# Fetching, transposing and preparing earlier in a fused attention and feed-forward block on one Trainium2 core

## The chip, the cores and the metric

The kernel runs on one core of a Trainium2 chip. The metric is device time in microseconds (us) of one launch. TensorE (PE in the profile) multiplies matrices, VectorE (DVE), ScalarE (ACT) and GpSimd (POOL) work on elements, and SyncE (SP) issues every DMA of this kernel.

## The reference

One transformer block on x of 2048 rows by 1024 columns, all in float32, with 16 heads of 64 columns and a feed-forward part of width 2752 whose weights are four-bit codes with a scale for each 64 entries:

```
x = x + layernorm(attention(layernorm(x), Wq, Wk, Wv, Wo))      # causal, rotary positions on q and k
x = x + layernorm(ffn(layernorm(x)))                            # ffn(x) = (silu(x Wg') * (x Wu')) Wd'
Wg, Wu, Wd = NF4[codes] * scales
```

## The kernel before, in words

Every large product is made of three float32r matmuls on a high and a low part of each operand (`split`: ACT copies the high part, DVE subtracts to get the low part). Rows of x go in four chunks `c` of 512 rows, and in 16 blocks `t` of 128 rows.

The first part is attention. `qkv(m, c, ...)` (L226) makes q, k and v of head pair m for chunk c: 3 products of 24 matmuls each (L236 to L238), with x transposed in `xs` and weights in `w`. After each product ACT copies it to `t1`. q and k get their rotation and go to DRAM (`qs`, `ks`); v is transposed by TensorE at once (`pv`, L250), split and stored to `vs` (L255). Chunk 0 of x is transposed straight into tiles `xc`; `make_x` (L213) transposes the other chunks, stores them to DRAM (`xd`), and `load_x` (L199) fetches all four tiles of a chunk when its first head pair begins. The 32 pairs (m, c) are called groups; the first four are made at the start, the others in `rest`.

Attention proper is a list of 640 units (h, J, kb): head h, chunk J of queries, block kb of 128 keys. For a unit TensorE makes the scores (`s`, L454 and L455), ACT takes the exponential (L458) and a copy (`pw`, L125), DVE subtracts (`pw`, L126), and three units later TensorE multiplies by v (`o`, L478 to L480). `maxima` (`mx`, L420, reduced on DVE at L426) runs ahead to give each row's maximum, which goes into q. The loads are put at steps: `load_q` 4J + 4 + 8 units or less before the head begins, `load_k` 8 units, `load_v` 5 units. When a head ends, `yl` (L484) takes the sums and products to DRAM (`at`).

The generator `rest` (L564) is the filler: its matmuls are drawn between those of the units until `FILL` is met, a table of how many should be spent by which step. A `yield GAP` ends the filler's turn in a step. When its groups are done, `rest` loads and splits the eight tiles of the output projection (`prep_wo`, L490: load `wof`, ACT copy L494, subtraction on DVE or POOL L495), and then projects the blocks t = 0 to 11 (`project_out`; `pj`, L529 to L531). `attended(t)` (L509) loads the heads' products (`af`) and the reciprocals of their sums (`rt`), multiplies and splits them (`ah`, `af`). `reciprocals(J)` (L500) fetches the 16 rows of sums of a chunk with eight DMAs and stores their reciprocals with eight. `residual` adds, normalizes, and the block's `y` goes to DRAM (`yd`).

The second part is the feed-forward: `fill_x2(t)` (L650) loads y and transposes it (`pt`, L153) into tiles `x2`, `gate_up` (L660) makes gate and up products (`bk`, L119 to L121), `gate_up_weights` (L323) and `looked_up` (L290) turn codes into weights (seven ACT lines, L307, and some eleven DVE operations per 512 columns), and `down` makes the last product.

On-chip memory is in slots of fixed size, named in `SLOTS`: for instance `f4` has four of 4 KB a partition (weights `wf` and `wof`, `hl`, `vo`, `af`, `ah`), `pw` three of 4 KB, `ol` one of 2 KB, `xc` four, `pa` six and `w` three of 8 KB. A tile waits until the one that had its slot is no longer read. The order of instructions is made in two steps. The functions above give a priority by the order in which they are called; the tile scheduler then orders each engine's instructions by these priorities and its own timeline of what is ready. TensorE's matmuls in the attention part are chained to the order written. Each engine, SP too, works its instructions in the order of the built program.

Of the kernel before, what the change touches and what calls it, by code (L numbers as in the profile page):

```python
# [21 lines left out]
E = 1024  # L22
D = 64
# [12 lines left out]
MOST = 16  # L36
LAG = 3

FILL = ((-12, 0), (14, 304), (130, 912), (290, 1520), (430, 2128), (438, 2128), (630, 2704))
# [19 lines left out]
def block_kernel(ctx, tc, x, wq, wk, wv, wo, gu_codes, gu_scales, d_codes, d_scales, cos_sin, out):  # L59
# [104 lines left out]
    at = [dram.tile([2 * KE, D + 1, 512], F32, tag=f"at{c}", name=f"at{c}") for c in range(NC)]  # L164
# [34 lines left out]
    def load_x(c):  # L199
        tiles = []  # L200
        for kp in range(4):
            tiles.append(slot("xc", [P, 4, 2, 2, P], FR, "xc"))
            load(f32(tiles[kp]), xd[c][:, kp])
        return tiles
# [8 lines left out]
    def make_x(c, t, xt):  # L213

        xs = slot("pa", [P, 4, 2, 2, P], FR, "xs")
        for g in range(0, KE, 4):
            pt = bank("T", "pt").rearrange("p (k n) -> p k n", k=4)
            for k in range(4):
                yield T.transpose(pt[:, k], xt[:, (g + k) * P : (g + k + 1) * P], ident)
            for k in range(0, 4, 2):  # L220
                split(xs[:, (g + k) // 2, 0], xs[:, (g + k) // 2, 1], pt[:, k : k + 2])
            if g:
                load(xd[c][:, :, t], f32(xs))
            yield GAP

    def qkv(m, c, ws, xs, tab, ramp=False, following=None):  # L226

        cs = slice(c * 512, (c + 1) * 512)
        for n in range(3):
# [16 lines left out]
            if n == 2:  # L246
                yield GAP
                pv = bank("T", "pv").rearrange("p (t n) -> p t n", t=4)
                for t in range(4):
                    yield T.transpose(pv[:, t, :], t1[:, t * P : (t + 1) * P], ident)  # L250
                vo = slot("f4", [P, 2, 4, 2, D], FR, "vo")
                src = pv.rearrange("p t (a d) -> p a t d", a=2)
                for a in range(2):
                    split(vo[:, a, :, 1], vo[:, a, :, 0], src[:, a])
                load(  # L255
                    vs[m][:, :, 4 * c : 4 * c + 4].rearrange("a p t n -> p a (t n)"),
                    f32(vo.rearrange("p a t l d -> p a (t l d)")),
                )
            else:
# [9 lines left out]
                else:  # L269
                    for a in range(2):  # L270
                        load(ks[m][a][:, :, cs].rearrange("a d s -> d a s"), f32(hl[a * D : (a + 1) * D]))
            yield GAP

# [10 lines left out]
    for m in range(STARTUP):  # L284
        ws[m + 2] = [None] * 3 if m + 2 <= STARTUP else None
        for _ in qkv(m, 0, ws[m], xs, tab, True, ws[m + 2] and (ws[m + 2], m + 2, ("w", "pa", "w", "w")[m])):
            pass
        done.add((m, 0))

    def looked_up(codes, s0, s1, rows, tags=None):  # L290

        if tags:
            c8, sc = (slot(tag, [P, 512], F32, "cs") for tag in tags)
        else:
            cs = slot("pw", [P, 2, 512], F32, "cs")
            c8, sc = cs[:, 0], cs[:, 1]
# [4 lines left out]
        l0 = slot("ol" if not tags else "t2", [P, 512], F32, "l0")  # L301
# [21 lines left out]
    def gate_up_weights(it, tags=None):  # L323
# [4 lines left out]
        def columns_of(k0):  # L328
# [4 lines left out]
                gu_codes[:, off : off + n], gu_scales[0:1, off : off + n], gu_scales[1:2, off : off + n], P, tags  # L333
# [137 lines left out]
    def weighted(u, h, J, kb):  # L471
# [11 lines left out]
        y = slot("pw", [D + 1, 512], F32, "yl")  # L483
        A.copy(y, o[: D + 1, :])  # L484
        load(at[J][h], y)
# [14 lines left out]
    def reciprocals(J):  # L500

        r = slot("ol", [P, D], F32, "sums")
        for a in range(8):
            load(r[16 * a : 16 * a + 16], at[J][:, D, a * D : (a + 1) * D])
        V.reciprocal(r, r)
        for a in range(8):
# [368 lines left out]
```

## Time and profile before

| | us |
|---|---|
| median of 3 runs | 3160.05 (3159.8 to 3160.71) |
| profiled execution, its own time | 3161.3 |
| its span | 3159.5 |
| TensorE busy (97%) | 3052.3 |
| DVE busy (66%) | 2097.3 |
| ACT busy (58%) | 1830.8 |
| POOL busy (17%) | 527.9 |

The page of the profile shows busy time per engine, the span cut in 40 slices of 79 us (a digit is the busy share in tenths; PEclk is the clock that TensorE was granted), and the costliest groups. The trace behind it can be asked for waits (who waited for whom), for stretches of time, and for single instructions. A matmul of 512 columns is shown with 0.39 us, but one starts every 0.23 us, since they overlap. The queues moved 554.71 MB, 176 GB/s over the span.

### The profile page before, as it was taken

Reading aid. Unit: us, or ns where it says so; the run is one execution under the profiler, and the core shown is the slowest. Engines: PE = TensorE matmul, PEld = TensorE weight load, DVE = VectorE, ACT = ScalarE, POOL = GpSimd, SP = SyncE. Lnnn points to the kernel's source line nnn. Section 1 sums busy time; section 2 is a strip of 40 time slices with the busy share of each in tenths; the row PEclk is TensorE's granted clock in tenths of the full one; section 3 lists DMA queues with packets and bytes.
Section 4 is the critical chain, followed back from the end, with each engine's and each line's share of the span. In section 5 each row is a group of like instructions: output and inputs, shape, how many; then the busy total and the mean of one; then the engine's idle time right before and its main releaser. Section 6 shows DMA issues by size and latency. Waiting matters only on the chain.

```text
span 3159.5 us, 41575 instructions
## 1 busy us (share of the span) xinstructions
PE 3052.3 (97%) x14272; PEld 2442.6 (77%) x14272; DVE 2097.3 (66%) x3809; ACT 1830.8 (58%) x3318; POOL 527.9 (17%) x430
## 2 busy tenths in 40 slices
PE   8989999999999997999989899999999999999998
PEld 6768777777777775777767788888888888888887
DVE  6646665766666665777776697667766679867322
ACT  3445565666666665666674586556655557657311
POOL 7534333232333321100101000000000000000000
PEclk9999999999999998999999999999999999999999
DMA  6977767766675656667535432222222235867785
GB/s 204 282 231 229 229 185 221 214 183 174 176 203 170 175 152 188 162 168 186 156 116 157 160 120 103 99 100 100 98 93 90 100 107 190 286 212 237 266 296 204
DMA packets 374100, 554.71 MB, mean 176 GB/s; under 512 B 25920, under 2 KB 238912, under 8 KB 358016
## 3 DMA queue, kind: packets, MB, share of 16 engines
q1 hardware_dynamic: 373888, 552.04, 56.8%
q8 instruction: 113, 1.85, 0.2%
q14 instruction: 99, 0.81, 0.1%
HBM read 410.12 MB, written 141.82 MB: 175 GB/s over the span
## 4 chain that ended last, share of the span: by engine, by line
PE 84%; DMA 6%; DVE 5%; ACT 2%; POOL 1%; issue 1%; SPq 1%; DVEq 0%; POOLq 0%; ACTq 0%
PE bk L119 14%; PE bk L120 14%; PE bk L121 14%; PE qkv L236 5%; PE qkv L237 5%; PE qkv L238 5%; PE mx L420 4%; PE s L454 4%; PE s L455 3%; PE o L479 3%; PE o L480 3%; PE o L478 3%; DMA af<-at 2%; PE pj L529 1%; PE pj L530 1%
## 5 line engine op out<-in xcount | busy, mean ns | idle before, releaser
L307 ACT ACTIVATE ln<-cs,bias 128x512 f32<-128x512 f32 x910 | 611.4, 718 | 119.0 <-DVE mp L313 41.5
L426 DVE TENSOR_REDUCE mxs<-mx 128x1 f32<-128x512 f32 (+3 forms) x640 | 386.4, 605 | 230.9 <-PE mx L420 127.7
L119 PE MATMUL bk<-x,wt 128*128 128x512 f32 x1376 | 536.2, 391 | 2.5 <-ACT x L125 2.4
L121 PE MATMUL bk<-x,wt 128*128 128x512 f32 x1376 | 536.3, 390 | 1.2 <-DVE wt L126 1.2
L120 PE MATMUL bk<-x,wt 128*128 128x512 f32 x1376 | 536.6, 390 | 0.0
L458 ACT ACTIVATE s<-s 128x512 f32<-128x512 f32 (+3 forms) x640 | 332.2, 520 | 286.2 <-PE s L455 164.3
L126 DVE TENSOR_TENSOR pw<-s,pw 128x512 fp32r<-128x512 f32 (+3 forms) x640 | 385.7, 606 | 142.0 <-ACT pw L125 137.6
L125 ACT CAST pw<-s 128x512 fp32r<-128x512 f32 (+3 forms) x640 | 333.3, 523 | 70.3 <-PE o L479 56.1
L182 POOL TENSOR_TENSOR w<-wf,w 128x512 fp32r<-128x512 f32 x192 | 250.8, 1317 | 650.1 <-ACT w L181 463.0
L137 POOL TENSOR_TENSOR rs<-ve,nhalf 128x1 f32<-128x1 f32 x64 | 39.4, 616 | 1786.5 <-DVE ve L135 1786.5
L236 PE MATMUL qkv<-xc,w 128*128 128x512 f32 x768 | 307.0, 401 | 1.7 <-ACT t L243 0.8
L237 PE MATMUL qkv<-xc,w 128*128 128x512 f32 x768 | 305.7, 398 | 0.0
L238 PE MATMUL qkv<-xc,w 128*128 128x512 f32 x768 | 304.1, 396 | 0.0
L119 PEld LDWEIGHTS bk<-x,wt 128*128 128x128 f32 x1376 | 258.9, 188 | 57.2 <-ACT x L125 2.9
L121 PEld LDWEIGHTS bk<-x,wt 128*128 128x128 f32 x1376 | 258.9, 188 | 55.2 <-DVE wt L126 1.6
L120 PEld LDWEIGHTS bk<-x,wt 128*128 128x128 f32 x1376 | 259.2, 188 | 53.8
L454 PE MATMUL s<-q,ka 128*128 128x512 f32 (+3 forms) x640 | 242.2, 378 | 21.4 <-DVE pw L126 21.1
L119 PE MATMUL bk<-wd,it 128*128 128x512 f32 x672 | 261.6, 389 | 1.2 <-DMA it<-ind 1.2
L420 PE MATMUL mx<-ka,q 128*128 128x512 f32 (+3 forms) x640 | 243.8, 383 | 18.4 <-DMA q<-qs 12.4
L120 PE MATMUL bk<-wd,it 128*128 128x512 f32 x672 | 261.5, 389 | 0.0
L121 PE MATMUL bk<-wd,it 128*128 128x512 f32 x672 | 261.3, 389 | 0.0
L478 PE MATMUL o<-pw,va 128*65 128x512 f32 (+3 forms) x640 | 235.8, 368 | 0.0
(126 smaller groups left out, 5436.7 us busy)
## 6 DMA issues: line engine op xcount, KB each, us to landing
it<-ind SPq DMA_DIRECT2D x84, 1024.0 KB
ind<-hl SPq DMA_DIRECT2D x84, 512.0 KB
va<-vs SPq DMA_DIRECT2D x160, 256.0 KB
cs<-in_gu_codes SPq DMA_DIRECT2D x86, 256.0 KB
cs<-in_gu_scales SPq DMA_DIRECT2D x172, 128.0 KB
wf<-in_wq SPq DMA_DIRECT2D x32, 512.0 KB
wf<-in_wk SPq DMA_DIRECT2D x32, 512.0 KB
wf<-in_wv SPq DMA_DIRECT2D x32, 512.0 KB
```

The costliest lines, as they stand in the source:

```text
L119: r = T.matmul(o, lhsT=w[:, 0], rhs=xx[:, 0], start=first, stop=False)
L120: T.matmul(o, lhsT=w[:, 0], rhs=xx[:, 1], start=False, stop=False)
L121: T.matmul(o, lhsT=w[:, 1], rhs=xx[:, 0], start=False, stop=last)
L125: A.copy(hi, src)
L126: V.tensor_tensor(lo, src, f32(hi), ALU.subtract)
L236: yield T.matmul(o, lhsT=w[k][:, 0], rhs=xx[0], start=k == 0, stop=False)
L237: yield T.matmul(o, lhsT=w[k][:, 0], rhs=xx[1], start=False, stop=False)
L238: yield T.matmul(o, lhsT=w[k][:, 1], rhs=xx[0], start=False, stop=k == KE - 1)
L307: A.activation(ln, c8, AF.Identity, bias=bias_of[ab], scale=ab[0])
L420: chain(T.matmul(s, lhsT=q[:, 0, j * P : (j + 1) * P], rhs=ka[:, b:e], start=True, stop=not diag))
L426: V.tensor_reduce(mx[:, j, i : i + 1], s, AX.X, ALU.max, negate=True)
L454: chain(T.matmul(s[:, cs], lhsT=ka[:, ks_], rhs=q[:, 0, cs], start=True, stop=False))
```

## The change

Six things change, with the same matmuls in all.

- `load_x(c, kps)` fetches part of a chunk. Two of the four tiles are fetched when head pair 6 of the chunk before begins, into slots given by `X_TAGS` that are free then; the other two and the table when the chunk's own first pair begins. Instead of ten pauses there are two, then 12 matmuls on the first two tiles, then three pauses.
- `qkv` no longer transposes v itself. It returns a generator `values`, which the next group runs after its first product (24 matmuls later).
- `prep_wo` runs in the last groups: tile 0 into `pa` at the last but one, tiles 1 to 3 into `w` after each product of the last, tiles 4 to 7 into `xc` after it, ahead of `attended(0)`.
- `at` is laid out `[D + 1, 2 KE, 512]`, so that the 16 rows of sums of a chunk are adjacent. One DMA fetches them and one stores the reciprocals.
- The last entry of `FILL` moves from step 630 to 643, and y of block 0 is fetched at step 634.
- In the second part, `x2` of chunks 2 and 3 is filled with a `gate_up` between the two. Some tiles change slots: `yl` from `pw` to `ol`, `xs` of `make_x` from one `pa` to two halves in `pw`, the first codes from `ol` and `t2` to `pw`, the sums to a tile of their own.

```diff
+X_TAGS = (("xc",) * 4, ("pa", "pa", "xc", "xc"), ("xc", "xc", "pa", "pa"), ("xc",) * 4)
-FILL = ((-12, 0), (14, 304), (130, 912), (290, 1520), (430, 2128), (438, 2128), (630, 2704))
+FILL = ((-12, 0), (14, 304), (130, 912), (290, 1520), (430, 2128), (438, 2128), (643, 2704))
-    at = [dram.tile([2 * KE, D + 1, 512], F32, tag=f"at{c}", name=f"at{c}") for c in range(NC)]
+    at = [dram.tile([D + 1, 2 * KE, 512], F32, tag=f"at{c}", name=f"at{c}") for c in range(NC)]
...
-    def load_x(c):
+    def load_x(c, kps):
         tiles = []
-        for kp in range(4):
-            tiles.append(slot("xc", [P, 4, 2, 2, P], FR, "xc"))
-            load(f32(tiles[kp]), xd[c][:, kp])
+        for kp in kps:
+            tiles.append(slot(X_TAGS[c][kp], [P, 4, 2, 2, P], FR, "xc"))
+            load(f32(tiles[-1]), xd[c][:, kp])
...
     def make_x(c, t, xt):
-        xs = slot("pa", [P, 4, 2, 2, P], FR, "xs")
         for g in range(0, KE, 4):
+            xs = slot("pw", [P, 2, 2, 2, P], FR, "xs")
...
-            if g:
-                load(xd[c][:, :, t], f32(xs))
+            load(xd[c][:, g // 2 : g // 2 + 2, t], f32(xs))
...
-            if n == 2:
-                yield GAP
-                pv = bank("T", "pv").rearrange("p (t n) -> p t n", t=4)
...
+            if after_n:
+                after_n(n)
             yield GAP
+            if n == 0:
+                yield from before
+
+        def values():
+            pv = bank("T", "pv").rearrange("p (t n) -> p t n", t=4)
+            for t in range(4):
+                yield T.transpose(pv[:, t, :], t1[:, t * P : (t + 1) * P], ident)
...
+            done.add((m, c))
+            yield GAP
+
+        return values()
...
     def reciprocals(J):
-        r = slot("ol", [P, D], F32, "sums")
-        for a in range(8):
-            load(r[16 * a : 16 * a + 16], at[J][:, D, a * D : (a + 1) * D])
+        r = small.tile([P, D], F32, tag="sums", name="sums", bufs=1)
+        load(r, at[J][D].rearrange("h (a d) -> (h a) d", a=8))
         V.reciprocal(r, r)
-        for a in range(8):
-            load(rcp[J][:, a * D : (a + 1) * D], r[16 * a : 16 * a + 16])
+        load(rcp[J].rearrange("h (a d) -> (h a) d", a=8), r)
...
     def rest():
...
             if m == 0:
                 while ("x", c) not in done:
                     yield GAP
-                xs_, tab_ = load_x(c), load_tab(c)
-                for _ in range(10):
+                xs_ = [*ahead, *load_x(c, range(len(ahead), 4))]
+                tab_, ahead = load_tab(c), []
+                for _ in range(2):
                     yield GAP
+            if m == KE - 2 and ("x", c + 1) in done:
+                ahead = load_x(c + 1, range(2))
+            if g == len(groups) - 2:
+                wot[0] = prep_wo(0, "pa")
...
+            def wo_after(n):
+                wot[n + 1] = prep_wo(n + 1, "w")
+
+            one = qkv(
+                m, c, w, xs_, tab_, False, None if last else (following, groups[g + 1][0], "w"), values, wo_after if last else None
+            )
+            if m == 0:
+                for _ in range(12):
+                    yield next(one)
+                for _ in range(3):
+                    yield GAP
+            values = yield from one
             w = following
+        for k in range(4, KE):
+            wot[k] = prep_wo(k, "xc")
+        yield from values
         ready = [attended(0)]
-        for k in range(KE):
-            wot[k] = prep_wo(k, "w" if k < 3 else "xc" if k < KE - 1 else "pa")
-        for _ in range(6):
+        for _ in range(8):
             yield GAP
...
+    put(634, 5, load_y, 0)
...
-    for c in range(2):
-        gate_up(*todo[1], c)
-    new_x2(2, ["w"] * 3 + ["pa"])
-    new_x2(3, ["xc"] * 4)
-    for t in range(8, NT):
-        fill_x2(t)
+    for c, tags in ((2, ["w"] * 3 + ["pa"]), (3, ["xc"] * 4)):
+        new_x2(c, tags)
+        for t in range(4 * c, 4 * c + 4):
+            fill_x2(t)
+        gate_up(*todo[1], c - 2)
```

## The prediction, made before the change was run

> **What bounds the kernel now.** I read the page's busy lines first, then TensorE's waits, then stretches of the trace around those waits.
>
> ```profile
> PE 3052.3 (97%) x14272; PEld 2442.6 (77%) x14272; DVE 2097.3 (66%) x3809; ACT 1830.8 (58%) x3318; POOL 527.9 (17%) x430
> ...
> PE   8989999999999997999989899999999999999998
> ...
> PEclk9999999999999998999999999999999999999999
> ```
>
> TensorE (PE) is the bound: 97% busy, nobody else over 66%. The change has the same matmuls, shape by shape, so it can gain only where TensorE waits, or works at a reduced clock. Both show in the early slices and in two dips, near 1200 us (the page's slice 16) and 1650 us (slices 21 to 23). The view of waits for TensorE (line, what it waited for, us in total, times, longest) says on what:
>
> ```profile
> PE s L454 <- DVE pw L126: 21.1, 23, 3.6
> PE mx L420 <- DMA q<-qs: 12.4, 1, 12.4
> ...
> PE pj L529 <- ACT wo L494: 8.4, 4, 5.2
> PE pt L153 <- DMA y<-yd: 6.6, 2, 4.0
> PE pv L250 <- ACT t L243: 5.7, 3, 2.6
> ...
> PE pt L153 <- DVE hl L678: 3.7, 1, 3.7
> ```
>
> Each is a few long waits, not a steady drip. Asked by stretch (start:end and length, busy and count of PE, PEld, DVE, ACT, POOL, granted clock, DMA share, GB/s):
>
> ```profile
> 76.00:128.00 52.00, 44.21 (x189) 35.47 (x188) 30.43 (x56) 18.23 (x40) 32.14 (x27) 0.88 0.93 271
> 204.00:229.00 25.00, 12.62 (x76) 10.85 (x75) 7.86 (x20) 9.96 (x25) 2.48 (x2) 0.73 0.93 305
> 506.00:524.00 18.00, 14.76 (x77) 10.86 (x75) 10.59 (x22) 11.65 (x27) 2.50 (x2) 0.91 1.05 364
> 1204.00:1249.00 45.00, 28.64 (x92) 18.01 (x91) 17.93 (x28) 19.04 (x30) 9.46 (x4) 0.70 0.78 209
> 1300.00:1600.00 300.00, 292.57 (x1391) 219.53 (x1389) 220.80 (x404) 198.14 (x351) 31.74 (x26) 1.00 0.62 164
> 1618.00:1654.00 36.00, 27.90 (x118) 18.91 (x116) 28.33 (x52) 31.14 (x59) 3.90 (x3) 0.91 0.38 116
> 1654.00:1668.00 14.00, 8.79 (x31) 6.71 (x32) 9.71 (x23) 6.83 (x18) 0.00 (x0) 0.52 0.43 133
> 1691.00:1699.00 8.00, 5.18 (x20) 4.06 (x19) 5.60 (x9) 4.78 (x9) 0.00 (x0) 0.79 0.93 221
> 1764.00:1798.00 34.00, 25.41 (x125) 20.19 (x124) 21.65 (x52) 20.33 (x48) 0.55 (x1) 0.85 0.61 203
> 1840.00:1920.00 80.00, 80.00 (x355) 66.26 (x354) 73.20 (x129) 60.47 (x97) 0.00 (x0) 1.00 0.35 119
> ```
>
> The last row is the yardstick: full clock, no gap, 80/355 = 0.225 us per 512-column matmul. Everything after 1800 us looks so and the change does not enter it, apart from the last waits of the output. In 1204:1249 only 92 matmuls ran, worth at most 92 x 0.225 = 20.7 us: at least 24 of 45 us are lost, of them 45 - 28.64 = 16.4 idle and the rest slow clock.
>
> [...] after a gap of 2.43 us before the `pv` transposes at 81.3 us, a matmul took 0.63 us, where before the gap it took 0.39. So a wait costs more than its length. [...] SP took 11.99 us, from 1217.38, for five `wof` issues. [...] `attended(0)` holds two of the four `f4` buffers while eight `wof` want the rest.
>
> **The change, part by part**, against the profiled span of 3159.5 us (3161.3 us with what lies around the span; the median of the runs is 3160.05, so the profiled execution is a usual one, and the saving is taken off the median).
>
> 1. *v behind the next product.* In 76:128 TensorE idles 52 - 44.21 = 7.8 us and the clock lacks 0.12 x 52 = 6.2 us. Two of the `pv` waits (2.4 and 2.6 us) lie here. With 24 other matmuls (5.4 us) between the copy of `t1` and its transposes, that copy is long done. What is late next is DMA, at 0.93 here. I take **-8** (ends 0 and -13).
>
> 2. *x a group ahead.* In 204:229 TensorE idles 12.4 us; with the slow clock after it some 15 are lost. SP was issuing four 1024 KB loads of x, the k stores and a weight load, so the q load of the next head went out late and took 5.72 us. Two of the four x loads now come earlier, and the order of instructions in the built program has 72 projection matmuls between units 20 and 30 where 24 stood: 48 x 0.225 = 10.8 us of cover. **-10** (-5 to -15). In 506:524, the next row, the same emptiness costs 3.2 idle and 1.6 of clock: **-4** (0 to -5). The third row gives nothing: between 600 and 1190 us TensorE waits 0.4 us in all.
>
> 3. *Projection weights in the last group.* Now each of the eight is a load (3.5 to 6.8 us), an ACT copy (1.04), and a DVE (1.22) or POOL (2.36) subtraction, in two buffers, with `pj` waiting. Moved, they stand in ACT's order between units 428 and 436, and `pj` starts after unit 440: at 2.1 us per unit (300 us for 143 units in 1300:1600) that is over 8 us of lead, before `attended(0)` takes its two buffers. ACT's 8 x 1.04 = 8.3 us then queue before the exponentials, which have room (ACT at 198 of 300). What stays is `ah`, which held ACT 4.07 us for the load of `rt`. Of 24: **-19** (-8 to -24).
>
> 4. *Filler up to unit 643, y of row block 0 early.* From 1618 to 1668 the 149 matmuls are worth at most 33.5 of 50 us: 16 lost. The built order now has 43 `pj` matmuls after unit 630 where 3 stood, 18 of them after the last unit, while y loads. But ACT is at 31 of 36 us there, so the stretch cannot shrink much; what it gives is 40 x 0.225 = 9 us of `pj` taken out of the earlier, full stretch. **-9** (-2 to -16).
>
> 5. *Sums adjacent.* Sixteen small DMAs (SP 3.56 and 3.55 us) become two, ahead of the `ah` that TensorE awaits in 1691:1699, where 2.8 + 1.7 are lost: **-3** (0 to -4.5). The rows of `at` lie 32 KB apart instead of 2; the pieces stay 2048 and 512 bytes, and `af` is loaded 48 matmuls ahead: 0.
>
> 6. *Row blocks 8 to 15 filled between products.* 1764:1798 loses 8.6 idle and up to 5.1 of clock; y of the last blocks stays the late thing. **-5** (+3 to -13).
>
> 7. *What it adds.* Two x loads per row start only when the old x is free; 2 MB at the 305 GB/s of 204:229 is 6.9 us, against 12 matmuls and three pauses. 2 us a row, **+6** (0 to +20). `xs` in the three `pw` buffers may hold ACT until its store lands: **+2** (0 to +10). ACT's copies before exponentials: **+1** (0 to +5). Twelve more xd issues on SP against 56 fewer small ones, and `yl` in `ol`, used once in 4 to 16 units: 0, as SP's pauses hide them.
>
> Sum: -8 -10 -4 -19 -9 -3 -5 +9 = -49, so a span of 3159.5 - 49 = 3110.5, and **3111** as a median (3160.05 - 49).
>
> **Rivals.**
> *The waits half come back* (x late at each row, `wof` late for ACT, DMA full at the start): only items 2, 3 and 4 at their low ends plus half of 7's: -5 -8 -2 -8 +2, about -20: **3140**. For it: DMA shares over 0.9 in three of the stretches. Against: the order gives each load more lead.
> *All goes*: each item at its far end, -90, less 5 added: **3075**. Against: DVE waits like the 21.1 us of `s` stay.
> *Slower: SP's one queue.* In the last group a `wof` at its head waits for a buffer while q, k and v of the next heads stand behind. k goes out 8 units ahead, 8 x 2.1 = 17 us. The hold seen is 12 us, so it hides. It decides from 17 us on, and each head that is then late costs what 204:229 lost, 15 us. Four heads are 60, more than the 49: 3160 + 60 - 49 = **3171**. Against it: four buffers turn over where two did.
> *No effect* would need TensorE's order unchanged, and the built order does differ.
>
> **How the numbers follow.** Forecast 0.70 (own range 3090 to 3132), half back 0.17, all goes 0.08, slower 0.05. The range 3076 to 3150 leaves out the slower case and the ends. Within 0.2% (6 us, about what a measurement of this kernel tells from no change) lies the far edge of the second case, 0.03: faster 0.92, same 0.03, slower 0.05.
>
> **What would show it.** Right: no `q<-qs` wait of 12 us near 205; `pv` waits gone; `wo` gone from TensorE's waits; a clock of 9 in slice 16; steady stretches after 1800 us unchanged. Step 2 fails if `qkv` waits for `xc`, step 3 if `s` waits while ACT waits for `wof`, step 4 if 1618:1668 still idles 13 us. The forecast is wrong if new waits of over 40 us appear.

## The result, and the profile after

The forecast was 3111 us, faster. The changed kernel takes 3170.62 us (median of 9 runs, 3163.15 to 3181.73) against 3162.39 for the kernel before (9 runs, 3159.8 to 3165.3): a ratio of 1.0029, 95% interval 1.0015 to 1.0042. It is slower by 0.3%.

The profiled execution of the changed kernel is its slowest, 3181.73 us with a span of 3180.0, 11 above its median. So the profile is used for what waits for what; sizes are taken from runs of kernels that differ in one part. First the busy lines of its page, and the rows of TensorE and its clock over the 40 slices:

```profile
PE 3059.7 (96%) x14272; PEld 2450.1 (77%) x14272; DVE 2092.3 (66%) x3809; ACT 1831.7 (58%) x3318; POOL 532.4 (17%) x430
...
PE   8799999999999998999997899999999999999998
...
PEclk9899999999999999999999999999999999999999
```

The dip at slice 16 has gone from the clock, as forecast, and half from TensorE's row (7 to 8). In its place slice 2 is lower in both, and the dip of slices 21 to 23 is still there. TensorE's waits (line, what it waited for, us in total, times, longest):

```profile
PE s L466 <- DVE pw L127: 36.2, 16, 6.1
PE mx L432 <- DVE xs L127: 11.0, 3, 6.9
PE mx L432 <- DVE mxs L438: 10.5, 8, 4.8
...
PE pt L154 <- DMA y<-yd: 8.0, 2, 4.5
PE pj L539 <- ACT ah L126: 7.5, 2, 5.3
PE pt L220 <- DVE mxs L438: 5.6, 2, 4.7
PE pv L269 <- ACT t L244: 3.8, 1, 3.8
```

The wait for `q` (12.4) and those for `wo` are gone. But `s` waits 36.2 us for `pw` where it waited 21.1, in fewer and longer waits, and `mx` waits 21.5 for DVE where it waited 4.2. Nothing here is slower work: DVE and ACT are as busy as before, to 5 us. Now the stretches of the prediction that changed most (start:end and length, busy and count of PE, PEld, DVE, ACT, POOL, clock, DMA share, GB/s):

```profile
76.00:128.00 52.00, 35.83 (x144) 28.61 (x143) 23.16 (x41) 13.95 (x31) 24.99 (x21) 0.80 0.82 238
204.00:229.00 25.00, 23.15 (x135) 19.45 (x134) 11.26 (x25) 12.78 (x29) 8.69 (x7) 1.00 0.83 245
506.00:524.00 18.00, 18.00 (x96) 14.38 (x95) 11.11 (x20) 11.95 (x24) 2.54 (x2) 1.00 0.94 308
1204.00:1249.00 45.00, 35.30 (x149) 24.95 (x149) 32.00 (x52) 31.22 (x57) 7.07 (x3) 0.89 0.75 206
1300.00:1600.00 300.00, 279.90 (x1290) 209.42 (x1289) 203.37 (x376) 183.20 (x328) 30.54 (x24) 0.96 0.56 155
...
1840.00:1920.00 80.00, 80.00 (x355) 66.24 (x354) 75.37 (x133) 63.54 (x101) 0.00 (x0) 1.00 0.35 119
```

204:229, 506:524 and 1204:1249 now hold 135, 96 and 149 matmuls for 76, 77 and 92: parts 2 and 3 do what they were to do (the two kernels reach the same unit up to 20 us apart, so a stretch does not hold quite the same work in both). The losses are in two places that the forecast had as a gain or as quiet: 76:128 lost 45 of its 189 matmuls, and 1300:1600, called steady, lost 101 of 1391, 23 us at 0.225 each.

### The profile page after: what moved, and what is told of

Read it like the earlier page. It is cut to its first block, busy times and chain, and to the rows that moved or that the text cites. A ratio compares the mean times of both kernels' runs of the same rounds, so it can differ in the third digit from the quotient of the medians.

```text
span 3180.0 us, 41427 instructions
## 1 busy us (share of the span) xinstructions
PE 3059.7 (96%) x14272; PEld 2450.1 (77%) x14272; DVE 2092.3 (66%) x3809; ACT 1831.7 (58%) x3318; POOL 532.4 (17%) x430
## 4 chain that ended last, share of the span: by engine, by line
PE 71%; DMA 4%; DVE 3%; ACT 1%; issue 1%; SPq 1%; POOL 0%; DVEq 0%; POOLq 0%; ACTq 0%
PE bk L121 14%; PE bk L122 14%; PE bk L120 14%; PE s L466 3%; PE mx L432 3%; PE s L467 3%; PE o L491 3%; PE o L490 3%; PE o L492 3%; PE qkv L237 2%; PE qkv L239 2%; PE qkv L238 2%; DMA af<-at 1%; PE pj L541 1%; PE pj L539 1%; PE pj L540 1%
## 5 line engine op out<-in xcount | busy, mean ns | idle before, releaser
L237 PE MATMUL qkv<-xc,w 128*128 128x512 f32 x768 | 310.5, 406 | 1.4 <-ACT t L244 0.9
L238 PE MATMUL qkv<-xc,w 128*128 128x512 f32 x768 | 308.2, 401 | 0.0
L239 PE MATMUL qkv<-xc,w 128*128 128x512 f32 x768 | 307.6, 401 | 0.0
L466 PE MATMUL s<-q,ka 128*128 128x512 f32 (+3 forms) x640 | 242.8, 379 | 36.2 <-DVE pw L127 36.2
L432 PE MATMUL mx<-ka,q 128*128 128x512 f32 (+3 forms) x640 | 246.8, 387 | 21.6 <-DVE xs L127 11.0
L467 PE MATMUL s<-q,kb 128*128 128x512 f32 (+3 forms) x640 | 236.6, 370 | 0.0
```

Of the source, the lines that this page charges most:

```text
L237: yield T.matmul(o, lhsT=w[k][:, 0], rhs=xx[0], start=k == 0, stop=False)
L238: yield T.matmul(o, lhsT=w[k][:, 0], rhs=xx[1], start=False, stop=False)
L239: yield T.matmul(o, lhsT=w[k][:, 1], rhs=xx[0], start=False, stop=k == KE - 1)
L432: chain(T.matmul(s, lhsT=q[:, 0, j * P : (j + 1) * P], rhs=ka[:, b:e], start=True, stop=not diag))
L466: chain(T.matmul(s[:, cs], lhsT=ka[:, ks_], rhs=q[:, 0, cs], start=True, stop=False))
```

## Where the time stands, by stage

For each kernel I read from the trace when the score matmul of each unit begins, and take from each stage's length what its matmuls need. For that I count 0.45 ns for each column streamed, as one matmul of 512 columns starts every 0.23 us, and transposes twice. The twice was assumed and is on the high side: in the kernel before four transposes of `pv` at 324.34 us took 0.36 us until the next matmul began (0.37 at 304.12 us in the changed one), 1.6 times their columns. That is some 0.1 us too much for four, and every kernel has as many. Quiet stretches then show 1 to 2 us in 20 units. What is left is lost to waits and slow clock, in us, one profiled execution each. The heads of the columns are units, and "to unit 0" is all before the first score. The kernels e1 to e15 are told below.

| | to unit 0 | 0 to 60 | 60 to 320 | 320 to 420 | 420 to 460 | 460 to 620 | 620 to end | ratio to before |
|---|---|---|---|---|---|---|---|---|
| before | 34.4 | 30.7 | 31.2 | 5.9 | 28.8 | 18.0 | 32.1 | 1 |
| changed | 43.8 | 26.6 | 37.5 | 5.9 | 17.1 | 40.8 | 29.8 | 1.0029 |
| e1, v at once | 31.6 | 21.6 | 28.1 | 6.0 | 14.2 | 18.2 | 22.4 | 0.9876 |
| e2, x at once | 40.5 | 34.0 | 40.1 | 5.9 | 16.6 | 33.9 | 34.7 | 1.0085 |
| e3, filler to 630 | 37.9 | 23.0 | 37.2 | 6.3 | 17.2 | 9.2 | 24.4 | 0.9923 |
| e6, e3 two units later | 38.9 | 22.2 | 38.5 | 5.9 | 16.8 | 24.3 | 29.1 | 0.999 |
| e9, e3 with v at once in the start | 29.5 | 20.2 | 32.2 | 6.8 | 16.3 | 7.5 | 32.5 | 0.9883 |
| e10, counts + 4 | 37.8 | 22.3 | 36.5 | 6.8 | 16.7 | 16.3 | 22.5 | 0.995 |
| e11, e1 with wo late | 30.4 | 20.5 | 31.8 | 5.9 | 24.6 | 17.6 | 21.0 | 0.9933 |
| e13, e1 with sums apart | 33.0 | 25.2 | 29.3 | 5.9 | 13.7 | 18.0 | 39.8 | 0.9933 |
| e15, e1 two units later | 32.2 | 23.5 | 27.9 | 5.9 | 12.6 | 24.2 | 39.1 | 0.9943 |

One execution is not the median. The row of the changed kernel is of its slowest execution: its stages add up to 59 us more than those of e1, where the medians differ by 49. The kernels e3, e4, e6 and e10 have the same start and lose 37.8 to 38.9 there, so some 6 of its 43.8 belong to that execution alone; e2, with the same projection, loses 33.9 in 460 to 620 for its 40.8.

The 15 kernels were run in four sets, each on another chip. The kernel before, run beside each set, took 3161.1, 3153.3, 3160.7 and 3160.6 us, so kernels of different sets are compared by their ratios to it (0.001 is 3.2 us). The intervals of single ratios reach 0.0008 to 0.0018 to each side; differences under some 6 us are not told apart.

## Which part costs: one part undone at a time (e1 to e4)

Theory H: the changed order puts instructions that wait for a DMA or for a slot at the head of ACT's or DVE's queue, and exponentials and `pw` stand behind them.

**e1.** `qkv` runs `values()` at once after its third product, and returns nothing to run later:

```diff
-            if n < 2:
+            if n == 2:
+                yield GAP
+                yield from values()
+            else:
...
-            if n == 0:
-                yield from before
```

> The changed kernel, but v is transposed at once after its product, as before. Theory H (work at the head of ACT's or DVE's queue waits for a DMA or a slot, and the exponentials and pw behind it are held): deferring v does its part of the loss only in the start, where in the changed kernel the first unit began at 143.8 us against 138.1; undone, it begins near 138 again, the pv waits of about 2.5 us return, and the time falls by 3 to 8 us against the changed kernel, to about 3165. Rival F (deferring v works as forecast, the loss is elsewhere): the time rises by 5 to 10, to about 3178. Rival N (no part matters for itself, the order as a whole is only unlucky): within 3 of the changed kernel.

3121.78 us, ratio 0.9876 (0.986 to 0.9893): 49 us faster than the changed kernel (1.0029 - 0.9876 = 0.0153, 48 us), six times what H allowed. With only this undone, the change is a gain of 1.2%. The table has it in the start (12 us, or 6 against the other kernels with the changed start), in 0 to 320 (14) and, unforeseen, in 460 to 620 (23) and behind (7), where no v is made any more.

**e2.** All of x when the chunk begins:

```diff
-                for _ in range(2):
+                for _ in range(10):
                     yield GAP
-            if m == KE - 2 and ("x", c + 1) in done:
-                ahead = load_x(c + 1, range(2))
...
-            if m == 0:
-                for _ in range(12):
-                    yield next(one)
-                for _ in range(3):
-                    yield GAP
...
-            xs = slot("pw", [P, 2, 2, 2, P], FR, "xs")
+        xs = slot("pa", [P, 4, 2, 2, P], FR, "xs")
```

> The changed kernel, but all four tiles of x are fetched when the chunk begins, into xc as before, with ten pauses, and xs of make_x is one tile in pa. Theory H: the halves of xs in pw hold ACT and DVE at units 0 to 60 (loss 8.5 and 6.4 us in ten units against 2.3 and 3.1), and the stretches at units 170 and 200 lose 4 each more; undone these 15 us come back, but units 20 to 30 lose their 11 us again (q awaited for about 12 us): a few us faster than the changed kernel, about 3166. Rival F (x ahead is a clear gain as forecast): 8 to 14 slower, about 3181. Rival N: within 3.

3188.02 us, 1.0085 (1.0072 to 1.0098): 18 us slower than the changed kernel. Rival F holds, H does not: x ahead, with the slots that came with it, is a plain gain. The long wait is back in TensorE's list:

```profile
PE mx L433 <- DMA q<-qs: 12.9, 1, 12.9
```

**e3.** The filler's last entry, and no early `y`:

```diff
-FILL = ((-12, 0), (14, 304), (130, 912), (290, 1520), (430, 2128), (438, 2128), (643, 2704))
+FILL = ((-12, 0), (14, 304), (130, 912), (290, 1520), (430, 2128), (438, 2128), (630, 2704))
...
-    put(634, 5, load_y, 0)
```

> The changed kernel, but the filler ends at unit 630 as before and y of block 0 isn't fetched early. Theory H: with the slower filler the ACT copy of the output projection (y) reaches the head of ACT's queue before the block before has stored its rows, which held ACT 15.1 us in three waits, and TensorE lost 26 us in units 470 to 610 against 6; undone, ACT's wait for x1d is gone, these units lose under 10, while 1618 to 1700 us loses some 6 more: about 10 faster than the changed kernel, 3160. Rival F (filler to 643 gains 9): 9 slower, 3180. Rival N: within 3.

3137.19 us, 0.9923 (0.991 to 0.9935): 33 us faster than the changed kernel, three times what H expected, and nearly all of it where H put it: 460 to 620 loses 9.2 for 40.8.

**e4.** `x1` in another slot:

```diff
-        residual(t, y, slot("pb", [P, E], F32, "x1"))
+        residual(t, y, slot("pw", [P, E], F32, "x1"))
```

> The changed kernel, but x1 of each block of the output projection takes a slot of pw (three) in place of one of the two of pb, so that y of the next block no longer shares its slots with it. Theory H: ACT's wait of y for the store (15.1 us in three) goes, and units 470 to 490 and 500 to 510 lose under 3 where they lost 8 and 5: 5 to 12 faster than the changed kernel, about 3161. Rival D (the stores and loads are late by themselves, whichever slot): the wait moves to x or rt, and the time is within 3.

3164.78 us, 1.0011 (0.9999 to 1.0022): about 6 faster, at the edge of what is told apart. Units 460 to 620 lose 21.9 for 40.8, but the stretch after unit 620 loses 46.4 for 29.8, with `pt <- DMA y<-yd` up from 8.0 to 18.4 us: the tiles in `pw` now stand against the `y` loads of the second part. Half of each theory, and no gain to keep.

## Units 460 to 620: the place of the projection against the heads

Why would both e1 and e3 remove the same loss? In the changed kernel, look at ACT around the longest wait (start, length, engine, line, operation; in brackets the idle time before and what ended it):

```profile
1319.27 0.58 ACT L126 CAST pw<-s 128x512 fp32r<-128x512 f32 x1
1327.29 0.58 ACT L542 COPY y<-pj 128x512 f32<-128x512 f32 x1 [7.43 <-DMA x1d<-x]
1327.77 0.59 ACT L470 ACTIVATE s<-s 128x512 f32<-128x512 f32 x1
```

The copy of the next block's `y` needs a `pb` slot whose rows are still on their way to `x1d`. It heads ACT's queue for 7.43 us, and the exponential behind it, which waits for nothing of its own, starts only then. SP's timeline of the same kernel, in the same columns, tells why the store is late:

```profile
1309.50 0.46 SPq L403 DMA_DIRECT2D kb<-ks  x1
1310.01 0.58 SPq L397 DMA_DIRECT2D ka<-ks  x1
1310.64 2.44 SPq L398 DMA_DIRECT2D q<-qs  x1
1313.12 0.76 SPq L399 DMA_DIRECT2D q<-qs  x1
1313.98 0.69 SPq L551 DMA_DIRECT2D x1d<-x  x1
```

The 512 KB of `x1d` are issued behind `kb`, `ka` and `q` of the next head (512, 1024, 128 and 256 KB, 1.9 MB) and have landed when ACT starts at 1327.29, 13.3 us after their issue. In SP's timeline of e3 (start, length, engine, line, operation) the same store goes out just ahead of them:

```profile
1300.95 0.34 SPq L551 DMA_DIRECT2D x1d<-x  x1
1301.40 1.15 SPq L414 DMA_DIRECT2D va<-vs  x1
1302.65 0.55 SPq L403 DMA_DIRECT2D kb<-ks  x1
1303.24 0.58 SPq L397 DMA_DIRECT2D ka<-ks  x1
```

There ACT copies `y` at 1306.27 with no wait, 5.3 us after the issue.

In this stage a head has 16 units, and its loads go out at every 16th step. A block of the projection has 48 matmuls. With the filler to 630 it is drawn at 576/192 = 3 a unit, so a block too has 16 units, and its place against the heads' loads is the same for all twelve blocks. To 643 it is 576/205 = 2.81, 17.1 units a block, and the place drifts. By units, `x1d` and the next `ka` stand at 461/465, 477/481, 493/497 in the kernel before, 463/464, 479/481, 495/496 in e3, but 464/464, 482/480, 500/497, 515/512 in the changed kernel: behind from the second block on.

That store is not all of it. ACT's waits for `x1d` end near units 488, 504 and 519, and with the first two go the losses of 7.7 us in units 480 to 490 and 5.0 in 500 to 510. Units 540 to 600 lose 22.6 us more (4.0 in e3), and there ACT waits for no `x1d`. One of these losses, 7.4 us in 590 to 600, can be read: `af`, the heads' products for the next block, is loaded just behind `kb` and `ka` (SP), DVE stands 6.63 us for it at the head of its queue, ACT then for DVE, and `pw` and the scores behind them:

```profile
1558.28 0.47 SPq L403 DMA_DIRECT2D kb<-ks  x1
1558.80 0.58 SPq L397 DMA_DIRECT2D ka<-ks  x1
1562.60 1.22 SPq L524 DMA_DIRECT2D af<-at  x2
```

```profile
1572.72 1.23 DVE L529 TENSOR_TENSOR rt<-af,rt 128x1024 f32<-128x1024 f32 x1 [6.63 <-DMA af<-at]
```

So the place bears on the projection's loads as well as on its stores. Nor is a store ahead of the loads enough: the kernel before has that in every block and loses 18.0 in this stage, for 9.2 in e3, with ACT waiting 39.0 us for `ah` where e3 waits 20.7.

Deferred v moves this place too. The start's last v goes to the filler, so the groups have 28 x 76 + 4 = 2132 matmuls there (72 matmuls and 4 transposes each), while `FILL` holds at 2128 from step 430 to 438; the last four transposes are left until 439, and the projection begins two units later (first `y` at unit 452, with v at once at 450). Theory P says that this place, not the rate and not v itself, is what costs in this stage.

**e6.** e3, with the last stretch of filler two units later (the end of `FILL`):

```diff
-(430, 2128), (438, 2128), (630, 2704))
+(430, 2128), (440, 2128), (632, 2704))
```

> The kernel with the filler to 630 (3137.2), but its last stretch begins and ends two units later (440 and 632): the same rate of 3 matmuls a unit, 48 to a block, so 16 units a block, as many as a head has. Theory P (phase): at 630 the store x1d of each block goes out one unit before the loads of the next head (units 463, 479, 495 against 464, 480, 496); two units later it stands behind those 1.9 MB in each block, y of the next block waits for it at ACT's head for 4 to 7 us, and TensorE loses 2 to 4 us a block: 20 to 40 slower, 3157 to 3177, with ACT's wait of y for x1d in 8 or more blocks. Rival R (the rate of 2.81 against 3 a unit is what matters): within 5 of 3137.

3151.0 us, 0.999 (0.9982 to 0.9998): 14 us more than e3, 21 by the ratios, so it falls at or just under the low end of P and outside R. ACT's waits in 1240:1650 of e6, with e3's having no such line:

```profile
ACT y L542 <- DMA x1d<-x: 22.1, 9, 4.9
```

Nine blocks wait, as P said; the price of one was less (units 460 to 620 lose 15 more, under 2 a block). The period is the same in both, so it is the place that costs this.

**e10.** The changed kernel with four more in the filler's counts:

```diff
-(430, 2128), (438, 2128), (643, 2704))
+(430, 2132), (438, 2132), (643, 2708))
```

> The changed kernel (1.0029 of before) with the filler's counts from step 430 on raised by 4: the start hands its last v to the filler, whose groups so have 2132 matmuls, and the 4 transposes of the last v are left over until step 439, with the projection behind them some two units later (first y at unit 452 against 450 with v at once, first x1d at 464 against 462). Theory P (phase): this gives the projection the place against the heads' loads that it has with v at once; ACT's wait of y for x1d falls from 15 to under 9 us, units 480 to 620 lose some 17 where they lost 38, and the time is 10 to 22 less, about 0.998 of before. Rival O (the loss there has another cause in the deferral): within 4 of 1.0029.

3143.41 us, 0.995 (0.9935 to 0.9965): **25 us faster than the changed kernel, for a 4 in a table**, and a little more than P expected. `x1d` now stands at 462, 478, 495, within a unit of its places in e1. ACT's waits in the stage have this line in the changed kernel:

```profile
ACT y L542 <- DMA x1d<-x: 15.1, 3, 7.4
```

and this one in e10:

```profile
ACT y L542 <- DMA x1d<-x: 7.3, 3, 3.3
```

The stage lost 40.8 (33.9 in e2) and loses 16.3; the gain is larger than the 8 us that the waits for `x1d` give back, so the store is not all that the place moves. The place still drifts: from the fourth block on `x1d` stands behind the loads here and in e1 as well (513/512, 531/528), a unit or two ahead of the changed kernel, and most of the loss is gone all the same. A unit or two decides, then, and not simply ahead or behind; why 560 to 570 loses 7.7 us in the changed kernel and 0.2 here was not taken apart.

**e15.** e1, moved two units the other way:

```diff
-(430, 2128), (438, 2128), (643, 2704))
+(430, 2128), (440, 2128), (645, 2704))
```

> The changed kernel with v at once (0.9876 of before), its last stretch of filler from 440 to 645 instead of 438 to 643: the projection two units later against the heads, where the changed kernel has it. Theory P (the place is the cause, not the deferral): the first x1d goes out at unit 464, ACT's wait of y for x1d rises from 8 to 13 us or more, units 480 to 620 lose over 28 where they lost 17, and the time is 10 to 27 longer, about 0.9935 of before. Rival (the place matters only with v deferred): within 4 of 0.9876.

3144.07 us, 0.9943 (0.993 to 0.9956): 21 slower than e1, as expected, with v at once. But the number came right for a reason that is only in part P's. 460 to 620 loses 24.2 for 18.2, short of the 28 that were expected of 480 to 620, and the wait for `x1d` is 10.6 us, less than the 13. The other 17 are lost after unit 620, where the projection's last blocks come later too. So the place costs with v at once as well, but only some 6 us of it are shown in the stage; e10 and e6 carry P.

**e5.** Both edits, that of e1 and that of e3:

> The changed kernel with both: v transposed at once, and the filler ending at 630 without the early y. The two undone alone gave 3121.8 and 3137.2 against 3170.6. Theory H2: two causes. One (slots of f4) costs some 25 us in the start, at the changes of rows and in the last group; the other (the projection's stores against the loads of the heads, units 480 to 610) some 25, which each of the two edits takes away by itself, since both move the projection against the heads. Together they then give less than the sum: about 3108 (3100 to 3115). Rival S (two independent costs): the sum, 3170.6 - 48.8 - 33.4 = 3088.

3124.77 us beside a before of 3153.34, 0.9907 (0.9893 to 0.992). Not the sum, so S falls, and H2 is right that both edits remove one thing: units 460 to 620 lose 7.4. But it is not below e1 either: what that stage gains, the end gives back (33.6 us after unit 620, for 22.4). By the medians e5 is 3 us above e1, by the ratios 10; the two sets do not settle which.

**e12.** e1, with `x1` in `pw` for blocks 0 to 11 only:

```diff
-        residual(t, y, slot("pb", [P, E], F32, "x1"))
+        residual(t, y, slot("pw" if beside else "pb", [P, E], F32, "x1"))
```

> The changed kernel with v at once (0.9876 of before), and x1 of blocks 0 to 11 in pw instead of pb. ACT's wait of y for x1d (8.1 us in 4) goes, units 580 to 610 lose 2 where they lost 7 to 9: 3 to 8 faster, about 0.9858 of before. Rival: in pw x1 collides with rt and the codes' tiles, and the time is the same or longer.

3129.18 us, 0.9901 (0.9883 to 0.9918): no gain, rather 8 slower. The waits for `x1d` are gone and the stage loses 14.0 for 18.2; the end loses 31.8 for 22.4, with TensorE waiting 10.1 us for `y`. As in e4, the wait moved.

## The start: a store, its own load, and what stands behind

**e8.** The kernel before, with v deferred and nothing else (the lines on `values` and `before` in the diff of the change):

```diff
-            if n == 2:
+            if n < 2:
...
+            if n == 0:
+                yield from before
```

> The kernel before with the deferral of v alone. Theory O: it costs here as well, the pv waits (5.7 us) go, weight loads wait for the stores of q and v, and the start and the changes of rows lose 10 to 25: 3170 to 3185 against 3161. Rival F (as forecast): 8 less, 3153. Rival X (it costs only beside the other parts): within 4 of 3161.

3170.51 us, 1.0054 (1.0041 to 1.0067): 17 slower. It costs by itself. Against the profile of the kernel before, which is of another set, it loses 6 us more in the start, 3 in units 0 to 20, 6 in 160 to 320 and 6 around the projection weights, and 7 less in 460 to 620. This profile is of its fastest execution, and its stages add up to only 5 us more, so they do not place all of the 17.

**e7.** e3, with the slot of `vo` taken just behind the third product:

```diff
+        vo = slot("f4", [P, 2, 4, 2, D], FR, "vo")
+
         def values():
...
-            vo = slot("f4", [P, 2, 4, 2, D], FR, "vo")
```

> The kernel with the filler to 630 (3137.2), v still deferred, but the f4 slot of vo is taken right after v's product, where the order of the slots was before; its transposes and stores stay behind the next product. Theory O (order of slots): deferring moved vo's turn in f4 behind hl of the next q, so that the weight load wf of v takes the slot of hl, and waits on SP for the store of q to land (13 us of such waits in the first 1240 us, none with v at once), with the loads behind it late; with the old turn these waits go, the first unit begins 3 to 6 us earlier, and the time comes within 6 of the kernel with both undone, which I put at 3108. Rival T (the later transposes and stores of v themselves, or the tile t1 held in t2 for longer): it stays at 3137 within 5.

3140.47 us, 0.995 (0.9937 to 0.9964): no gain, T's side. But the edit did not do what it was for: weight loads still waited 5.1 us for stores of q between 40 and 145 us (5.2 in e3). So it is no verdict on the order of the slots. What its list of SP's waits did show, as that of e3 (10.9 us in 3, the longest 5.1), is a larger one, of the loads of v:

```profile
SPq L415 <- DMA vs<-vo: 10.9, 3, 5.4
```

In SP's timeline of e3, around the longest of its own:

```profile
96.60 0.56 SPq L256 DMA_DIRECT2D qs<-hl  x1
97.20 0.67 SPq L274 DMA_DIRECT2D vs<-vo  x1
102.96 0.92 SPq L414 DMA_DIRECT2D va<-vs  x2
103.97 0.45 SPq L174 DMA_DIRECT2D wf<-in_wq  x1
```

v is stored at 97.20, and the next issue is the load of the same v for the first heads. It waits at SP's head for the landing, 5.1 us with nothing issued; behind it stands a weight load. ACT then comes to the copy of those weights, and behind it stand `xs` copies for which TensorE waits (`mx <- DVE xs`). ACT's timeline of e3:

```profile
103.30 0.36 ACT L126 CAST xs<-pt 128x256 fp32r<-128x256 f32 x1
109.64 1.14 ACT L182 CAST w<-wf 128x512 fp32r<-128x512 f32 x2 [5.98 <-DMA wf<-in_wq]
110.68 0.70 ACT L126 CAST xs<-pt 128x256 fp32r<-128x256 f32 x2
```

From 100 to 112 us TensorE ran 6 matmuls at half clock (0.50, the row of e3 under e9 below). SP issues nothing for 5.1 us, from 97.87 to 102.96. ACT stands 5.98 us ahead of copies that need no weights: the transposes for them had all ended by 105.00 us (in the trace of e3 the last four begin at 103.88 and take 1.12), and the copies begin at 110.68. In the traces of the kernel before and of the changed kernel nothing passes what stands ahead of it on its engine: all 14272 matmuls, 3316 instructions of ACT, 3745 of DVE and 427 of POOL, and the DMAs of SP (1568 and 1524) start in the order of the built program, line by line.

**e9.** e3, with v at once in the four groups of the start only:

```diff
-            behind = yield from qkv(m, 0, ws[m], xs, tab, True, following, behind)
+            yield from (yield from qkv(m, 0, ws[m], xs, tab, True, following))
```

> The kernel with the filler to 630 (0.9923 of before), with v at once in the four groups of the start only; the other 28 groups defer v. Theory Q (SP's queue): in the start the deferred store of v stands right ahead of the load of the same v for the first heads, which waits at SP's head until the store has landed (59.8 to 66.0 and 103.2 to 108.7 us in the changed kernel), and the weight load behind it comes 10 us late, for which ACT, then DVE and TensorE stand (4 matmuls between 100 and 110 us). With v at once there, the first unit begins at 134 to 136 instead of 138 to 144, units 0 to 20 lose 4 to 5 where they lost 10.5, and the time is 6 to 12 less, about 0.9895 of before. Rival A (the loss of the start comes from the other parts, or is given back in units 20 to 80): within 4 of 0.9923.

3122.41 us, 0.9883 (0.9867 to 0.99): 13 to 15 faster than e3, a little more than Q expected. The stretch 100:112 in e3 (columns as in the stretches above):

```profile
100.00:112.00 12.00, 1.47 (x6) 1.10 (x6) 4.22 (x8) 3.25 (x8) 5.18 (x5) 0.50 0.77 266
```

and in e9:

```profile
100.00:112.00 12.00, 9.13 (x48) 7.37 (x46) 6.25 (x14) 5.24 (x12) 6.98 (x6) 1.00 0.99 322
```

48 matmuls for 6. SP's wait for `vs` is 4.4 us for 10.9, and unit 0 begins at 133.2 us for 137.9. The edit also takes the start's last four transposes out of the filler, so it is not the queue alone that is tried: units 290 to 300 lose 0.7 for 8.0 (point 1 of the account below has why), and the end loses 8 more. Units 0 to 20, which were to fall to 4 or 5, still lose 9.7. That is the deferred v of the filler's first groups, for e5, which differs from e9 in the 28 groups alone, loses 3.9 there; but e5 loses 19.3 in units 20 to 60 and e9 10.5. In sum the 28 groups that still defer v cost nothing that these runs can tell: e9 is as fast as e1, and no slower than e5.

## The other parts, with the loss off them (e11, e13, e14)

**e11.** e1, with all eight `prep_wo` after the groups, as before:

```diff
-            if g == len(groups) - 2:
-                wot[0] = prep_wo(0, "pa")
...
-        for k in range(4, KE):
-            wot[k] = prep_wo(k, "xc")
...
         ready = [attended(0)]
+        for k in range(KE):
+            wot[k] = prep_wo(k, "w" if k < 3 else "xc" if k < KE - 1 else "pa")
```

> The changed kernel with v at once (0.9876 of before), but the projection weights made after the groups, as before. Early preparation as forecast, at the size that the traces show (units 430 to 460 lose 14 with it and 29 without): 10 to 18 slower, about 0.992 of before. Rival: ACT's copies of wo, wherever they stand, cost the exponentials as much: within 4 of 0.9876.

3137.35 us, 0.9933 (0.9917 to 0.9949): 18 slower than e1. Early preparation is worth what was forecast; units 420 to 460 tell 10 of it.

**e13.** e1, with `at` in its old layout and the sums in eight loads and eight stores:

```diff
-        load(r, at[J][D].rearrange("h (a d) -> (h a) d", a=8))
+        for a in range(8):
+            load(r[16 * a : 16 * a + 16], at[J][:, D, a * D : (a + 1) * D])
...
-        load(rcp[J].rearrange("h (a d) -> (h a) d", a=8), r)
+        for a in range(8):
+            load(rcp[J][:, a * D : (a + 1) * D], r[16 * a : 16 * a + 16])
```

> The changed kernel with v at once (0.9876 of before), with at in its old layout and the sums fetched and stored by 32 small DMAs of 4 KB a chunk pair as before. Forecast item 5: 0 to 4.5 slower, 3 taken, 0.9886. Rival (the layout with rows 32 KB apart costs the loads of af as much as the sums gain): within 1, or faster.

3140.46 us, 0.9933 (0.9917 to 0.995): 18 slower, four times the upper end. All of it is after unit 620 (39.8 for 22.4). SP's timeline of e13:

```profile
1623.87 0.55 SPq L498 DMA_DIRECT2D at<-yl  x1
...
1626.86 3.57 SPq L517 DMA_DIRECT2D sums<-at  x8
...
1632.40 3.55 SPq L520 DMA_DIRECT2D rc<-sums  x8
...
1636.52 1.30 SPq L531 DMA_DIRECT2D rt<-rc  x2
```

and in e1:

```profile
1618.46 0.54 SPq L498 DMA_DIRECT2D at<-yl  x1
...
1621.34 0.32 SPq L516 DMA_DIRECT2D sums<-at  x1
...
1624.62 0.32 SPq L518 DMA_DIRECT2D rc<-sums  x1
1626.14 1.27 SPq L529 DMA_DIRECT2D rt<-rc  x2
```

From the store of the last head to the load of `rt` it is 12.65 us, and 7.68 with two DMAs: 5 us on the chain that the prediction had as 3. The other 13 are lost later in the same stretch, where `x1d`, `y` and `yd` stand behind these on SP; I have not taken them apart, and that they are late for this reason is not shown.

**e14.** e1, with row blocks 8 to 15 filled after both products, as before:

```diff
+    for c in range(2):
+        gate_up(*todo[1], c)
+    new_x2(2, ["w"] * 3 + ["pa"])
+    new_x2(3, ["xc"] * 4)
+    for t in range(8, NT):
+        fill_x2(t)
-    for c, tags in ((2, ["w"] * 3 + ["pa"]), (3, ["xc"] * 4)):
...
```

> The changed kernel with v at once (0.9876 of before), with row blocks 8 to 15 filled after both products as before. Forecast item 6: 5 slower (3 faster to 13 slower), about 0.989, with the stretch behind the last unit losing some 20 where it lost 15. Rival (y of the last blocks is the late thing, whatever stands before it): within 2.

3128.28 us, 0.9894 (0.9879 to 0.9909): 6 slower, where 5 was forecast, at the edge of what is told apart. Behind unit 639 it loses 18.7 for e1's 15.0.

No combination beats e1 beyond its interval. The changed kernel with v transposed at once, 1.2% faster than the kernel before, is the version to keep.

## Why the prediction was wrong, point by point

1. *v behind the next product: -8, ends 0 and -13.* **This step failed.** It costs 48 us (e1). The working looked at TensorE's side, where it was right: the long waits of `pv` shrank from 5.7 us to 3.8. It named DMA as what is late next and priced nothing for it, and its bad end was 0 without a reason.

   The runs show two costs in its place. The DMA moves with the copy: the store of v goes out later, and in the start its own load, next on SP, waits for the landing with the weights behind it (10.9 us in three waits of e3, 4.4 in one of e9; v at once in the start alone gives 13 us back, e9, of which 8 before unit 0). And four transposes cross the end of the groups and push the projection two units on against the heads' loads (25 us, e10).

   The other 10 or so lie in units 160 to 320, which lose 12 more than in e1, at two places. At 290 to 300 (8.3 us for 1.2) ACT stands 5.84 us for weights `wf` whose load went out behind `kb` and `ka` (864.97 us, behind 863.68 and 864.34); in e1 it goes out ahead of `kb` (840.09, ahead of 844.47) and ACT does not wait. This goes with the start's v (0.7 in e9), so it is in e9's 13 as well, and the three amounts are not to be added. At 170 to 180 (5.4 for 1.0) e9 still loses 6.5, so it is of the groups' own v; its cause stays open.
2. *x a group ahead: -14, with +8 of added waits under 7.* Right in mechanism, too small: undone together they cost 18 us (e2), where 6 were forecast; the wait for `q` alone is 12.9 us. TensorE never waited for `xc`.
3. *Projection weights in the last group: -19.* Right: 18 (e11). ACT does wait for `wof` at the head, 10.2 us, with `s` behind it; this was priced at 1 and is in the 18. `s` waiting while ACT waits for `wof` was named as the sign that this step fails; it came, and the step gained.
4. *Filler to 643: -9.* In the changed kernel it is a loss of 33 (e3), by the place of the projection: the drift of 17.1 units a block does harm from the place that deferred v gives it, and much less from two units before (e10). With v at once it is a gain of 3 to 10 (e1 against e5, at the edge of what is told apart). The price was right for a place that the change itself took away. The sign named for this step's failing, 13 us of idle time in 1618:1668, did not come (3.2): the loss was elsewhere.
5. *Sums adjacent: -3.* Too small by a factor of six (e13): the nearest wait was 2.8 us, but 5 us go on the chain to `rt` alone. That the rest is what stands behind those 16 DMAs on SP is likely and not shown.
6. *Row blocks 8 to 15: -5.* Right (e14).
7. *Additions: +9.* Not measured by itself; 8 of it are in e2, 1 in e11.

Without item 1 the sum is -41, or 3119 us. The kernel without item 1 took 3121.78, 39 less than the kernel before beside it. So one term made the sign. But that agreement is luck in part: undone one at a time, items 2 to 6 cost 18, 18, 3 to 10, 18 and 6 us, 63 or more together, and not 39. They do not add up, or something that was not tried takes 24 back.

Two readings in the working were loose. `s` waiting for `pw` (21.1 us in 23 waits) is a drip, not a few long waits. In the rival "half back" the second -8 is of no item that its words name (5 and 6 together are 8), and +2 is not half of item 7.

The rivals: "slower, SP's one queue" gave 3171, and 3170.62 came, but by another way. Its place was the last group, with `q` late; no `q` is late there. SP's head is part of the cause, in the start and with v. "Half back" and "all goes" fell. Of the signs named, no wait for `q` near 205, `wo` gone from TensorE's waits, slice 16 at full clock and quiet stretches after 1800 all came true, and the time was still longer: they were signs that parts 2 and 3 work, and none looked at the stages called quiet.

## What to carry to other kernels

When a step is moved, follow its DMAs on their queue as well: what is issued next, and whether it is the load of the very data just stored (here up to 5.1 us with nothing issued, e3). Where a filler runs beside periodic work, its period and its place are quantities of their own; a few matmuls more or less upstream can move its loads and stores against a burst of other loads (here four transposes did, 25 us, e10). Equal periods only fix the place; try which place is good (at a period of 16 units this stage lost 9.2 us in e3 and 24.3 in e6, two units later). And before a loss is put to a part, undo the parts one at a time: here four of six were gains, the filler's a small one at most, and one hid them.

## What was not expected of the hardware

The wait for a 512 KB store issued behind 1.9 MB of loads ended 13.3 us after its issue; issued just ahead of them, the same store had landed in under 5.3 us. With waits of TensorE of up to 4.8 us scattered over 1300:1600, the mean clock there was 0.96 for 1.00 before, and some 23 us of matmuls were lost where idle time rose by 13 (from 7 to 20). And the kernel before ran at 3153.3 us in one set and at 3161 in the other three, on other chips. An 8 us difference across sets can so be the set's own.
